# Third feed-forward: the rows of four fixed expert quads go through DRAM instead of through products of zeros and ones

## The chip, the core and the metric

The kernel runs on one core of one Trainium2 chip. The metric is the device time of one execution in microseconds; the median of three runs is compared. The engines are PE (matrix products; PEld loads its weights), DVE (vector), ACT (scalar and activation), POOL (GpSimd, which also issues the gathers and scatters by index) and SP (which issues most loads).

## What is computed

Four layers, each a cross-attention with a context and then a feed-forward, on 512 tokens of 256 features, all in float32. The change is in the feed-forward of the third layer, a mixture of eight experts in which each token goes to the one with the highest score:

```python
x = hidden_states.reshape(-1, 256)              # 512 tokens, normed
route = jax.nn.sigmoid(x @ router_w)            # 8 experts
max_ind = jnp.argmax(route, axis=1)
max_prob = jnp.take_along_axis(route, max_ind[:, None], axis=1)
for e in range(8):
    mask = (max_ind == e)[:, None]
    h = jax.nn.silu(x @ gate_w[e]) * (x @ up_w[e])          # inner width 512
    out = out + jnp.where(mask, h @ down_w[e], 0.0)
out = out * max_prob
# and around it: x = x + tanh(g_ffn[2]) * out
```

The fourth layer's cross-attention and feed-forward follow, and read x.

## The kernel before

**Slots.** The tokens of the third feed-forward are put into 768 slots, six quads of 128. Quads 0 to 3 (slots 1 to 512) are the fixed ones: each expert owns 64 slots, two blocks of 32, whatever the routing. Tokens beyond an expert's 64 go to blocks of 32 in quads 4 and 5, whose experts (`owners`) are only known when the counts are. `slot` holds each token's slot number from 1 on. Gathering tokens into slots is a product of a matrix of zeros and ones (`there`) with the normed tokens (L1233).

**A quad.** `l2_up(q)` does the gate and up products (L1396: four blocks of 32 rows side by side, 32 matmuls), silu on ACT (L1403) and the hidden product on DVE (L1405). `l2_turn` transposes the hidden rows (L634) and copies them out of PSUM (L195 on DVE and L197 on ACT in turn). `l2_down(q)` does the down products (L1417, 32 matmuls) into a PSUM tile `acc2`. `dn2` and `gu2` hold the eight down and eight gate-up weights; `home(q, j)` says which one a block uses.

**Back to tokens.** `l2_down` cuts the result into two parts[...]: DVE masks off the low bits (L1425), ACT copies the upper part (L1427), DVE takes the difference (L1428). `l2_mask(q)` (L1433) compares the row of slot numbers with the quad's own slots, which gives a matrix of zeros and ones; `l2_back(q)` (L1441) multiplies it with both parts, eight matmuls a quad, and all six quads accumulate into the two PSUM tiles `y`. `l3_stats(n)` then adds `y` times `c2` (the probability times the layer's gate) to row tile n of x on DVE (L276, the helper `add_to_x`) and starts the next norm.

**Order.** The loop over q runs up(q), mask and down of q - 1, turn of q, back of q - 2. The products on PE keep the order of the text (`inline(..., pe_line)`). DVE's order list was cleared just before this stage (`line.clear()`), so on DVE, ACT, POOL and SP a scheduler that runs at build time orders the instructions by the text and by when it takes their inputs to be ready; `behind(i, j, ...)` forces i after j on one engine. Each engine then executes its own list strictly in order, and waits at the head of it.

**Loads.** The weights of quads 4 and 5 overwrite those of the fixed quads: after up(q) SP loads the gate-up weights `gu2[2q]` and `gu2[2q+1]` (1 MB each, L1401), and after down(q) the down weights `dn2[2q]` and `dn2[2q+1]` (512 KB each, L1421). Then come the weights of the last feed-forward (`sh3`, `gu3`, `dn3`, L102) and its `shd` rows (L1476, L1477), which wait for a memset on POOL (L1475). Earlier, at 364.66 us, POOL writes zeros into the two DRAM tables `xg` and `yg` (L1038, L1039) that the last feed-forward uses to scatter (helper at L1635) and gather rows.

Of the kernel before, what the change touches and what calls it, by code (L numbers as in the profile page):

```python
# [17 lines left out]
F32 = mybir.dt.float32  # L18
F32R = mybir.dt.float32r
I32 = mybir.dt.int32  # L20
U8 = mybir.dt.uint8
AF = mybir.ActivationFunctionType
ALU = mybir.AluOpType
AX = mybir.AxisListType

P = 128
NT = 4
D = 256
# [9 lines left out]
QUADS = 6  # L38
# [12 lines left out]
def flamingo(ctx: ExitStack, tc: tile.TileContext, a: dict, out: bass.AP):  # L51
    nc = tc.nc

    def pool(name, bufs, space=None):
        kw = {} if space is None else {"space": space}
        return ctx.enter_context(tc.tile_pool(name=name, bufs=bufs, **kw))
# [3 lines left out]
    q2 = pool("q2", Q2)  # L60
    q1 = pool("q1", 4)
    small = pool("small", 6)
# [37 lines left out]
    def load(half, name):  # L100
        rows, cols = a[name].shape
        nc.sync.dma_start(half[0:rows, 0:cols], a[name])  # L102
        return half[0:rows, 0:cols]
# [67 lines left out]
    dram = pool("slots", 1, bass.MemoryType.DRAM)  # L171
    xg = dram.tile([E * CAP, D + 1], F32, name="xg")
    yg = dram.tile([2 * T, D], F32, name="yg")
    tg = const.tile([P, 8], F32, name="tg")

    nc.scalar.activation(tg[:, 0:1], eps_ln, AF.Sqrt)
# [8 lines left out]
    def behind(i, j, reason):  # L185

        tc.add_manual_dep(i.ins, j.ins.name, mybir.DependencyInfo(
            mybir.DependencyClass.NoSync, mybir.DependencyReason.DATA), reason=reason)
# [24 lines left out]
    def inline(i, line=line):  # L213
        if line:
            if line[-1] is not None:
                behind(i, line[-1], "in the order of the text")
            line[:] = [i]
        return i
# [49 lines left out]
    def mm(shape=None):  # L268
        return ps_mm.tile(shape or [P, 512], F32, tag="mm", name="mm")

    def chain(dst, pairs):
        for i, (lhsT, rhs) in enumerate(pairs):
            inline(nc.tensor.matmul(dst, lhsT=lhsT, rhs=rhs, start=(i == 0), stop=(i == len(pairs) - 1)), pe_line)  # L273

    def add_to_x(n, acc, scalar, cols=slice(0, D)):
        return inline(nc.vector.scalar_tensor_tensor(x[:, n, cols], acc, scalar, x[:, n, cols], ALU.mult, ALU.add))  # L276
# [202 lines left out]
    def l0_finish(n, den, mixed):  # L479
        r = q1.tile([P, D], F32, tag="q1", name="r0")  # L480
        inline(nc.vector.reciprocal(r, den))
        sums.append(mixed[:, 1, :])
        inline(nc.vector.tensor_mul(mixed[:, 0, :], mixed[:, 0, :], r))
        add_to_x(n, mixed[:, 0, :], gx(0))
        return r
# [4 lines left out]
    mixed, acc, es, stats, sums = {}, {}, {}, {}, []  # L490
    for s in range(18):
        n = s // 4
        if s < 16:
            es[s] = l0_scores(n, s // 2 % 2, s % 2)
        if 1 <= s <= 16:
            m, i, half = (s - 1) // 4, (s - 1) // 2 % 2, (s - 1) % 2
# [27 lines left out]
        if s % 4 == 1 and s > 1:  # L524
            den = l0_exchange(mixed[n - 1], n == 2, n == 4)
            r = l0_finish(n - 1, den, mixed[n - 1])
# [328 lines left out]
    for h in range(16):  # L855
# [9 lines left out]
        for b in range(B):  # L865
# [34 lines left out]
            if hl and g < 3:  # L900
                n = 2 * (hl - 1) + b
# [133 lines left out]
    zero = q2.tile([P, D + 1], F32, tag="q2", name="zero")  # L1035
    nc.gpsimd.memset(zero, 0.0)
    nc.gpsimd.iota(zero[:, D : D + 1].bitcast(I32), pattern=[[0, 1]], base=4096, channel_multiplier=0)
    nc.gpsimd.dma_start(xg.rearrange("(g p) d -> p g d", p=P), zero.unsqueeze(1).to_broadcast([P, E * CAP // P, D + 1]))  # L1038
    nc.gpsimd.dma_start(yg.rearrange("(g p) d -> p g d", p=P), zero[:, 0:D].unsqueeze(1).to_broadcast([P, 2 * NT, D]))  # L1039


    w2 = ffn1[3]
# [148 lines left out]
    def rtile(shape=(P, NT, E), dtype=F32):  # L1191
        return small.tile(list(shape), dtype, tag=f"r{len(shape)}", name="route", bufs=12)
# [37 lines left out]
    def gather2(dst, k, cols, tiles=range(NT)):  # L1230
        for n in tiles:
            for h in (xh, xl):
                inline(nc.tensor.matmul(dst, lhsT=h[:, n, k * P : (k + 1) * P], rhs=there[n][:, cols],  # L1233
                                        start=(n == 0 and h is xh), stop=(n == NT - 1 and h is xl)), pe_line)
# [99 lines left out]
    slot = rtile((P, NT))  # L1334
# [37 lines left out]
    c2 = const.tile([P, NT], F32, name="c2")  # L1372
    inline(nc.vector.tensor_scalar_mul(c2, top, gf(2)))
    line.clear()
    row = q2.tile([P, T], F32, tag="q2", name="row")

    def second_rows():
        p = mm([P, 2, SL - 512])
        for k in range(2):
            gather2(p[:, k, :], k, second)  # L1380
        for k in range(2):
            nc.scalar.copy(xsT[k][:, second], p[:, k, :])
        p = mm()
        chain(p, [(ones_r, diag.rearrange("p n t -> p (n t)"))])
        nc.scalar.copy(row, p)

    def home(q, j):

        return 2 * q + j // 2 if q < 4 else 4 * (q - 4) + j

    def l2_up(q):
        pa, pb = mm(), mm()
        for w, ps in ((0, pa), (1, pb)):
            for k in range(2):
                for j in range(4):
                    inline(nc.tensor.matmul(ps[j * BLK : (j + 1) * BLK, :],  # L1396
                                            lhsT=xsT[k][:, (4 * q + j) * BLK : (4 * q + j + 1) * BLK],
                                            rhs=gu2[home(q, j)][:, w * 1024 + k * 512 : w * 1024 + (k + 1) * 512], start=(k == 0), stop=(k == 1)), pe_line)
        if q < 4:
            for i in (2 * q, 2 * q + 1):  # L1400
                nc.sync.dma_start(gu2[i], a["l2_gu_all"][bass.ds(owners[i], 1), :, :].rearrange("e p c -> (e p) c"))  # L1401
        s = q2.tile([P, T], F32, tag="q2", name="silu")
        nc.scalar.activation(s, pa, AF.Silu)  # L1403
        h = q2.tile([P, T], F32, tag="q2", name="h2")
        nc.vector.tensor_mul(h, s, pb)  # L1405
        return h

    def l2_turn(h):
        hT = q2.tile([P, 4, P], F32, tag="q2", name="hT2")
        transposed(h, hT)  # L1410
        return hT

    def l2_down(q, hT):
        acc = ps_tr.tile([P, D], F32, tag="tr", name="acc2")
        for c in range(4):
            for j in range(4):
                inline(nc.tensor.matmul(acc[j * BLK : (j + 1) * BLK, :], lhsT=hT[:, c, j * BLK : (j + 1) * BLK],  # L1417
                                        rhs=dn2[home(q, j)][:, c * D : (c + 1) * D], start=(c == 0), stop=(c == 3)), pe_line)
        if q < 4:
            for i in (2 * q, 2 * q + 1):  # L1420
                nc.sync.dma_start(dn2[i],  # L1421
                                  a["l2_dn_all"][bass.ds(owners[i], 1), :, :].rearrange("e p c -> (e p) c"))

        top = q1.tile([P, D], F32, tag="q1", name="top2")
        nc.vector.tensor_scalar(top.bitcast(I32), acc.bitcast(I32), -4096, None, ALU.bitwise_and)  # L1425
        o = q2.tile([P, 2, D], F32R, tag="q2", name="o2")
        nc.scalar.copy(o[:, 0, :], top)  # L1427
        nc.vector.tensor_sub(o[:, 1, :], acc, top)  # L1428
        return o

    def l2_mask(q):
        back = q2.tile([P, T], F32R, tag="q2", name="back")
        nc.vector.tensor_scalar(back, row, own[:, q : q + 1], None, ALU.is_equal)  # L1433
        return back

    def l2_back(q, o, back, y):
        for n in range(NT):
            for i in range(2):


                inline(nc.tensor.matmul(y[n // 2][:, n % 2, :], lhsT=back[:, n * P : (n + 1) * P], rhs=o[:, i, :],  # L1441
                                        start=(q == 0 and n % 2 == 0 and i == 0),
                                        stop=(q == QUADS - 1 and n % 2 == 1 and i == 1)), pe_line)

    y = [ps_acc.tile([P, 2, D], F32, tag="acc", name="y2") for _ in range(2)]
    hTs, os, backs = {}, {}, {}
    for q in range(QUADS + 2):
        if q < QUADS:  # L1450
            h = l2_up(q)
        if q == 0:
            second_rows()
        if 1 <= q <= QUADS:
            backs[q - 1] = l2_mask(q - 1)
            os[q - 1] = l2_down(q - 1, hTs.pop(q - 1))

        if q == 4:
            w = pair(0, "sh3")
            sh = [load(w[:, k, :], f"l3_sh{k}") for k in range(2)]  # L1460
            w = pair(3, "gu3")
            gu3 = [load(w[:, k, :], f"l3_gu{k}") for k in range(2)]
        if q == 5:
            w = pair(4, "gu3")
            gu3 += [load(w[:, k, :], f"l3_gu{2 + k}") for k in range(2)]
            w = pair(5, "dn3")
            dn3 = [load(w[:, k, :], f"l3_dn{k}") for k in range(2)]
        if q < QUADS:
            hTs[q] = l2_turn(h)
        if q >= 2:  # L1470
            l2_back(q - 2, os.pop(q - 2), backs.pop(q - 2), y)
    pe_line.clear()
    late = pair(1, "late").rearrange("p s c -> p (s c)")
    shd = late[:, 0 : 6 * D].rearrange("p (c d) -> p c d", d=D)
# [310 lines left out]
    hs, hTs = {}, {}  # L1785
# [14 lines left out]
    rows = []  # L1800
    for n in range(NT):
        o = q2.tile([P, 2, D], F32, tag="q2", name="o3g")
# [680 lines left out]
```

## Time and profile before

| what | before |
|---|---|
| time, median of 3 runs (lowest to highest) | 583.55 us (582.22 to 584.46) |
| the profiled execution: its own time | 583.24 us |
| its span, first to last instruction | 581.5 us |
| mean granted clock of PE | 0.993 |
| busy in the span: PE, DVE, ACT, POOL | 550.4, 319.3, 229.9, 138.5 us |
| moved by DMA | 60.19 MB, 104 GB/s over the span |
| third feed-forward, first up product to first addition to x | 448.69 to 492.69 us |

A line of a profile names the engine, the line of the kernel, the operation and what it writes and reads (`out<-in`). In a timeline the first two numbers are start and duration in us, and a bracket at the end gives the idle time ahead of the instruction and what ended it. In the chain of waits each piece is what the next one waited for. GB/s stand in 40 equal slices of the span, 14.5 us each.

### The profile page before, as it was taken

How to read it: one execution, taken by the hardware profiler on the slowest of the kernel's cores; microseconds unless marked ns; L12 is line 12 of the kernel's file. 1: busy time of each engine (PE TensorE's matmuls, PEld its weight loads, DVE VectorE, ACT ScalarE, POOL GpSimd, SP SyncE). 2: the span in 40 equal slices, each digit the busy share in tenths (PEclk: the TensorE clock that was granted, in tenths of full speed). 3: DMA queues.
4: the chain of work that ended last, by engine and by line, in shares of the span. 5: the costliest groups of instructions: out<-in, count | busy, mean ns of one | idle time of the engine just before them, and what ended most of it. 6: DMA issues, size and time to landing. Idle time of an engine off the chain costs nothing.

```text
span 581.5 us, 8641 instructions
## 1 busy us (share of the span) xinstructions
PE 550.4 (95%) x3296; PEld 395.9 (68%) x3296; DVE 319.3 (55%) x731; ACT 229.9 (40%) x468; POOL 138.5 (24%) x233
## 2 busy tenths in 40 slices
PE   8988899989999999999999999999999999899995
PEld 6544575658888888788888887557766446884454
DVE  6979654284557455664545477314467434563323
ACT  6857544554344444534344531420332211432320
POOL 3887153131103011211101113102012000252150
PEclk9979999999999999999999999999999999999999
DMA  7900300000000400030003325932030799704013
GB/s 304 402 4 16 131 0 0 2 0 2 0 1 0 145 0 2 2 144 1 0 8 138 145 73 220 363 114 117 0 144 3 284 422 417 195 36 122 18 44 122
DMA packets 16071, 60.19 MB, mean 104 GB/s; under 512 B 2685, under 2 KB 5956, under 8 KB 12390
## 3 DMA queue, kind: packets, MB, share of 16 engines
q1 hardware_dynamic: 13974, 54.75, 25.4%
q0 software_dynamic: 1472, 4.28, 2.0%
q10 hardware_dynamic: 576, 0.53, 0.3%
q8 instruction: 28, 0.46, 0.3%
q14 instruction: 21, 0.17, 0.1%
HBM read 54.75 MB, written 5.25 MB: 103 GB/s over the span
## 4 chain that ended last, share of the span: by engine, by line
PE 74%; DVE 10%; POOL 5%; DMA 5%; ACT 3%; issue 2%; SPq 1%; POOLq 0%; ACTq 0%; DVEq 0%
PE mm L273 22%; PE acc L273 18%; PE mm L594 8%; PE mm L596 4%; PE mm L1396 4%; PE q L594 2%; PE mm L1729 2%; POOL tern L356 2%; PE acc L1417 2%; DMA w<-in_l_gate 2%; DVE x L276 1%; PE outT L680 1%; PE acc L1751 1%; PE q L596 1%; DVE signs L363 1%
## 5 line engine op out<-in xcount | busy, mean ns | idle before, releaser
L273 PE MATMUL mm<-qT,kT 128*128 128x256 f32 x256 | 61.0, 381 | 0.2 <-DVE kT L600 0.2
L273 PE MATMUL acc<-e,v 128*128 128x256 f32 x256 | 60.4, 379 | 0.0
L587 POOL TENSOR_TENSOR h_parts<-w,h_top 128x256 fp32r<-128x256 f32 x28 | 22.6, 808 | 150.9 <-PE acc L273 85.5
L273 PEld LDWEIGHTS mm<-qT,kT 128*128 128x128 f32 x256 | 48.0, 189 | 9.7 <-ACT oT L764 1.6
L273 PEld LDWEIGHTS acc<-e,v 128*128 128x128 f32 x256 | 48.4, 189 | 7.7
L753 ACT ACTIVATE e<-mm 128x512 f32<-128x512 f32 x64 | 38.0, 596 | 26.0 <-PE mm L273 25.8
L756 DVE TENSOR_TENSOR t<-e,e 128x512 f32<-128x512 f32 x32 | 22.1, 690 | 36.2 <-ACT e L753 36.2
L450 ACT ACTIVATE e<-s 128x512 f32<-128x512 f32 x64 | 33.0, 607 | 13.9 <-PE s L446 9.9
L227 POOL TENSOR_TENSOR rstd<-mv,eps_ln 128x1 f32<-128x1 f32 x30 | 6.2, 206 | 101.9 <-DVE mv L226 101.9
L273 PE MATMUL mm<-xT,ffn 128*128 128x512 f32 (+1 forms) x80 | 28.0, 509 | 1.3 <-ACT xT L1006 1.3
L273 PE MATMUL acc<-w,oT 128*128 128x256 f32 x112 | 27.2, 386 | 2.1 <-ACT oT L764 2.1
L594 PE MATMUL mm<-ctx_top,h_parts 128*128 128x512 f32 x56 | 27.2, 485 | 1.1 <-ACT h_parts L586 1.1
L599 ACT ACTIVATE v<-mm 128x512 f32<-128x512 f32 x24 | 14.3, 597 | 34.3 <-PE mm L596 34.3
L600 DVE SCALAR_TENSOR_TENSOR v<-mm,v 128x512 f32<-128x512 f32 x24 | 16.6, 691 | 18.7 <-ACT v L599 18.7
L276 DVE SCALAR_TENSOR_TENSOR x<-acc,gsum,x 128x256 f32<-128x256 f32 x56 | 24.1, 479 | 4.9 <-PE acc L273 4.9
L446 PE MATMUL s<-w_q,ctx_nat 32*128 32x256 f32 x256 | 23.9, 427 | 2.8 <-ACT e L450 2.0
L273 PEld LDWEIGHTS acc<-w,oT 128*128 128x128 f32 x112 | 20.7, 190 | 6.3 <-ACT oT L764 3.7
L599 ACT ACTIVATE kT<-mm 128x512 f32<-128x512 f32 x28 | 16.7, 598 | 20.6 <-PE mm L596 20.6
L764 ACT COPY oT<-acc 128x256 f32<-128x256 f32 x32 | 11.9, 373 | 32.4 <-PE acc L273 32.4
L273 PEld LDWEIGHTS mm<-xT,ffn 128*128 128x128 f32 x80 | 15.0, 190 | 13.6 <-issue 11.0
L594 PE MATMUL mm<-v_parts,ctx_top 128*128 128x512 f32 x48 | 22.1, 459 | 1.8 <-ACT e L753 1.8
L600 DVE SCALAR_TENSOR_TENSOR kT<-mm,kT 128x512 f32<-128x512 f32 x28 | 19.3, 689 | 7.1 <-ACT kT L599 7.1
(394 smaller groups left out, 1157.9 us busy)
## 6 DMA issues: line engine op xcount, KB each, us to landing
gu<-in_l_gu_all SPq DMA_DIRECT2D x16, 1024.0 KB, 7.0
w<-in_l_all SPq DMA_DIRECT2D x4, 2048.0 KB, 13.3
dn<-in_l_dn_all SPq DMA_DIRECT2D x4, 1024.0 KB, 6.3
dn<-in_l_dn_all SPq DMA_DIRECT2D x8, 512.0 KB, 9.7
gu<-in_l_gu SPq DMA_DIRECT2D x4, 704.0 KB, 11.7
ctx_nat<-in_ctx SPq DMA_DIRECT2D x4, 512.0 KB, 13.4
ctxT<-in_ctxT SPq DMA_DIRECT2D x4, 512.0 KB, 5.3
sh<-in_l_sh SPq DMA_DIRECT2D x2, 704.0 KB, 8.6
```

The source lines that it names most:

```text
L273: inline(nc.tensor.matmul(dst, lhsT=lhsT, rhs=rhs, start=(i == 0), stop=(i == len(pairs) - 1)), pe_line)
L276: return inline(nc.vector.scalar_tensor_tensor(x[:, n, cols], acc, scalar, x[:, n, cols], ALU.mult, ALU.add))
L446: in_turn(nc.tensor.matmul(ps[j][:, k, :], lhsT=ctx_nat[rows, b, hf, c * P : (c + 1) * P], rhs=qm[rows, n, i, :], start=True, stop=True))
L450: exps.append(nc.scalar.activation(es[j], ps[j], AF.Exp))
L587: nc.gpsimd.tensor_sub(dst[1], src, t)
L594: inline(nc.tensor.matmul(same, lhsT=left(i, k), rhs=right(i, k), start=(k == 0 and i == 0), stop=(k == 1 and i == 1)), pe_line)
L596: inline(nc.tensor.matmul(cross, lhsT=left(2, k), rhs=right(2, k), start=(k == 0), stop=(k == 1)), pe_line)
L599: nc.scalar.mul(dst, cross, -EPS * scale)
L600: return inline(nc.vector.scalar_tensor_tensor(dst, same, (1.0 + EPS) * scale, dst, ALU.mult, ALU.add))
L753: nc.scalar.activation(e, s, AF.Exp)
L756: nc.vector.tensor_add(t, es[0], es[1])
L1396: inline(nc.tensor.matmul(ps[j * BLK : (j + 1) * BLK, :], lhsT=xsT[k][:, (4 * q + j) * BLK : (4 * q + j + 1) * BLK], rhs=gu2[home(q, j)][: ...
```

## The change

The results of quads 0 to 3 no longer go back through masks and products. ACT copies each quad's `acc2` to SBUF, POOL writes its 128 rows (1 KB each) into a new DRAM table `ys`, and after the fourth quad POOL issues four gathers, one for each row tile of 128 tokens, by the index `static` (slot number less one; tokens without a fixed slot get row 512, which holds zeros). DVE adds the four gathered tiles to x with `add_to_x`, forced behind the hidden product of quad 5. Quads 4 and 5 keep masks and back products; back(4) is split in halves, one ahead of down(5) and one after it. The down loads of the last quads are moved in the text: four after down(2) and four after down(3), instead of two after each of the first four. The table's zero row is written beside the other zeros.

```diff
+    ys = dram.tile([5 * P, D], F32, name="ys")
...
+    nc.gpsimd.dma_start(ys[4 * P : 5 * P, :], zero[:, 0:D])
...
+    static = small.tile([P, NT], I32, tag="static", name="static", bufs=1)
+    nc.vector.tensor_scalar(static, slot, -1.0, 512.0, ALU.add, ALU.min)
...
-        nc.vector.tensor_mul(h, s, pb)
+        product[:] = [nc.vector.tensor_mul(h, s, pb)]
         return h
...
-        if q < 4:
-            for i in (2 * q, 2 * q + 1):
+        if q in (2, 3):
+            for i in range(4 * q - 8, 4 * q - 4):
                 nc.sync.dma_start(dn2[i],
                                   a["l2_dn_all"][bass.ds(owners[i], 1), :, :].rearrange("e p c -> (e p) c"))
+        if q < 4:
+            o = q1.tile([P, D], F32, tag="q1", name="o2s")
+            nc.scalar.copy(o, acc)
+            nc.gpsimd.dma_start(ys[q * P : (q + 1) * P, :], o)
+            return
...
+    def static_rows():
+        for n in range(NT):
+            r = q2.tile([P, D], F32, tag="q2", name="y2s")
+            nc.gpsimd.indirect_dma_start(out=r, out_offset=None, in_=ys[:, :],
+                                         in_offset=bass.IndirectOffsetOnAxis(ap=static[:, n : n + 1], axis=0),
+                                         bounds_check=5 * P - 1, oob_is_err=False)
+            fixed.append(r)
...
-    def l2_back(q, o, back, y):
-        for n in range(NT):
+    def l2_back(q, o, back, y, tiles=range(NT)):
+        for n in tiles:
             for i in range(2):
...
-                                        start=(q == 0 and n % 2 == 0 and i == 0),
+                                        start=(q == 4 and n % 2 == 0 and i == 0),
...
-    for q in range(QUADS + 2):
+    for q in range(QUADS + 1):
         if q < QUADS:
             h = l2_up(q)
         if q == 0:
             second_rows()
+        if q == QUADS:
+            l2_back(4, os[4], backs[4], y, (0, 1))
         if 1 <= q <= QUADS:
-            backs[q - 1] = l2_mask(q - 1)
+            if q > 4:
+                backs[q - 1] = l2_mask(q - 1)
             os[q - 1] = l2_down(q - 1, hTs.pop(q - 1))
+            if q == 4:
+                static_rows()
...
+        if q == 5:
+            for n, r in enumerate(fixed):
+                behind(add_to_x(n, r, c2[:, n : n + 1]), product[0], "rows come late")
         if q < QUADS:
             hTs[q] = l2_turn(h)
-        if q >= 2:
-            l2_back(q - 2, os.pop(q - 2), backs.pop(q - 2), y)
+        if q == QUADS:
+            l2_back(4, os[4], backs[4], y, (2, 3))
+    l2_back(5, os[5], backs[5], y)
     pe_line.clear()
```

## The prediction

> **What bounds the kernel now.** I read the page's engine table first, then the slices, then the chain of waits through the stage that the change touches, and last the instructions and transfers of that stage.
>
> ```profile
> PE 550.4 (95%) x3296; PEld 395.9 (68%) x3296; DVE 319.3 (55%) x731; ACT 229.9 (40%) x468; POOL 138.5 (24%) x233
> ...
> GB/s 304 402 4 16 131 0 0 2 0 2 0 1 0 145 0 2 2 144 1 0 8 138 145 73 220 363 114 117 0 144 3 284 422 417 195 36 122 18 44 122
> ```
>
> PE is busy nearly everywhere, but the three slices of 284, 422 and 417 GB/s (451 to 494 us) are this stage, and there the transfers are full too. Two resources run at their limit at once; a step taken off one helps only as far as the other allows. The chain through the stage (start, duration, what):
>
> ```profile
> 466.88 0.95 PE y L1441 x8
> 467.83 3.57 PE mm L1396 x32
> 471.40 1.73 PE acc L1417 x32
> 473.13 0.58 PE tr L634 x4
> 473.71 0.95 PE y L1441 x8
> ...
> 480.55 0.95 PE y L1441 x8
> 481.50 3.75 PE mm L1396 x31
> ...
> 485.28 0.20 PE mm L1396
> 485.48 1.93 PE acc L1417 x28
> 487.41 0.59 PE tr L634 x4
> 487.99 0.95 PE y L1441 x8
> 488.94 1.86 PE acc L1417 x32
> 490.81 1.15 PE y L1441 x8
> 491.95 0.12 PE tr L1489 x2
> 492.07 0.59 PE y L1441 x4
> 492.69 0.50 DVE x L276
> ```
>
> A quad is 3.57 (up) + 1.73 (down) + 0.59 (turn) + 0.95 (back) us of PE without a gap. The last quad's up takes 3.75 + 0.20 instead of 3.57, and the timeline names why: its last weights had only just landed.
>
> ```profile
> 482.06 2.28 PEld L1396 LDWEIGHTS mm<-gu,xsT 128*32 128x32 f32 x25 [0.48 <-DMA gu<-in_l_gu_all]
> ```
>
> So PE has no more than about half a microsecond over the weights. The stage ends at 492.69 us, when DVE adds the first finished row tile to x; everything later follows from that moment. I price the change by where this moment goes.
>
> **What is removed.** The back products of quads 0 to 3: 32 matmuls, 4 x 0.95 = 3.8 us, all on the chain. On DVE four masks (0.48), four cuts and four differences (0.42 each), 5.3 us; DVE idles over 4 us before each hidden product, so that is worth nothing. The ACT cast (0.41) becomes a copy of the same size: nothing.
>
> **What PE alone would do.** Without the three backs ahead of it the chain reaches up(5) early: up(3) 466.88 to 470.45, down(2) to 472.2, turn to 472.8, up(4) to 476.3, down(3) to 478.1, turn to 478.7, against 481.50 now (2.85 us).
>
> **The weights that move.** All eight down loads of the last two quads (0.33 to 0.50 us of SP each) now stand behind the gate-up loads of quads 2 and 3: four after down(2), four after down(3); no load goes. Bytes, at the 0.42 MB/us of the full slices, with 1.7 us from issue to first data (issue 452.36, data from about 454.1): gu(4,5), issued at 464.6 as now, flows 466.3 to 471.3. gu(6,7), issued at 470.45, flows 472.2 to 477.2. The four first down loads (2.1 MB), issued at 472.2, end at 482.2, the last four at 487.2. The new traffic shares the same engines: four writes and four gathers of 131 KB, 1.05 MB or 2.5 us. I give 0.8 us of it to the loads ahead of down(4) (483) and all to the last (490). So up(5) no longer waits, but down(4) starts at 483 instead of 482.2, and down(5) has no weights before 490, where today it starts at 488.94. The 3.8 us of PE are eaten here: even with nothing else late, down(5) runs 490 to 491.9, its cut and difference (from the end of down(5) at 490.8 to 491.8 today, 1.0 us) give 492.8, half a back (0.59) gives 493.4: +0.7. If SP keeps today's order of readiness instead (the loads of 304.07 us went out ahead of loads that stand before them in the text), gu(7) lands at 482 as now plus up to 1 us for the writes: between -0.3 and +0.7. I take +0.7.
>
> **The added path.** Quad 3's rows go: down(3) ends 478.1, ACT copy 0.41, POOL issue at 478.6, landing, then four gathers that wait for it, one every 1.28 us (the scatters of 518.96, 520.26, 521.53 us), landing, then four additions on DVE (0.48 to 0.50 each). The unknown is the landing of a POOL transfer in saturated engines. On quiet engines scatters of the same 128 rows land in:
>
> ```profile
> xg<-late,goes POOLq DMA_INDIRECT x8, 2.7
> ```
>
> The upper end is the 1 MB of zeros at 364.66, beside gate-up loads:
>
> ```profile
> yg<-zero POOLq DMA_DIRECT2D x1, 1024.0 KB, 13.8
> ...
> q0 software_dynamic: 563, 2.23, 57.8%
> q1 hardware_dynamic: 581, 1.67, 43.2%
> ```
>
> The last two lines are the 10 us from 371: the software queue got more than half of full engines, so it isn't starved, and most of the 13.8 us are eight times the rows. The landing is nearer the low end. **The rule:** the Trainium skill, page "DMA: Bandwidth & Descriptors", section "Anatomy of one DMA — SWDGE (gpsimd) path", fits 2.0 us + bytes/436 GB/s, 2.3 us here; its section "Latency and other measured facts" puts memory access at 0.2 us on average but 2 us at high load, which would make it about 4.1 (estimate of mine from the two). By the first alone: write 480.9, last gather issued 484.9, landed 487.2, rows in x by 487.7. By the second, and by the trace's 2.7 plus a share of the load, I take 4.0: write 482.6, gathers issued 482.7 to 486.5, last landing 490.5, rows in x by 491.1. The loaded value decides, since the slices say 420 GB/s throughout. No row shows a gather; it is bounded by 2.4 us (fastest scatter) and 8 (half the zeros' time, with something over).
>
> **What waits behind it.** The additions are held only behind the hidden product of quad 5 (about 483.1). Nothing in the code holds them behind the cut of down(4), and the program's order on an engine is by readiness in places: the product of L1489 stands after the last back in the text and runs ahead of it at 491.95; POOL's copy of L1568 ran at 487.73, ahead of norms that precede it. So I expect DVE to meet at least some additions before the cut of quad 4. DVE then stands until the rows land. Behind it: cut and difference of quad 4 (491.1 to 492.0), PE's first half of back(4) (0.48, to 492.5), which the new text puts ahead of down(5), so down(5) to 494.35, cut and difference to 495.35, half a back to 495.95. Against 492.69 that is **+3.3 us**. If the additions stand behind the difference of quad 4, they finish at 491.1 beside the wait for weights: the +0.7 above.
>
> **At nothing.** One index instruction on DVE (0.17 us, like L1345) in a gap. One more zero transfer (about 1.0 us of POOL, 128 KB): POOL idles 27.60 us from 366.8. The first three row writes (1 us of POOL each): POOL idles 43.8 us here. The memset L1475 and, after it, SP's load of shd move behind the gathers, from 487.5 to at most 488; its rows are first read at 564.4 (the shared products of L273), over 70 us of cover. If POOL's gathers ran past 495, norms of the next stage would wait up to 5.1 us (4 x 1.28): that is in the third case.
>
> **The rivals.** (1) DVE stands ahead of quad 4's cut: +3.3, from +1.2 (landing 3.2) to +6.5 (5.5). For: the gaps filled by readiness. Against: text order puts the cut first. It decides once the last row lands after about 487. (2) Additions after quad 4's difference, weights the limit: -0.4 to +2.5, centre +0.7. For: 422 GB/s. (3) The software queue is slow under load, 6 to 8 us a landing, twice in a row: +7 to +11. For: 13.8 us for the zeros. Against: 57.8% of the engines. (4) The other side: the saving arrives. The additions stay out of the way and loads keep ahead (the first down loads fill the gap at 460 us and gu(6,7) comes before the rest), so down(4) ends 484.0, back(4) follows at 484.9, down(5) 485.4 to 487.3, first addition at 488.8: -3.9, or -1.5 if the last down loads land at 487. It decides as soon as 1 us less of loads than today's lies ahead of each down. Against: the sum of bytes, which grows. A change that leaves the back products in place is excluded by the diff: the products start at quad 4.
>
> **How the numbers follow.** The sum is against the profiled execution, span 581.5, 583.24 us with what lies around it; the median of the three runs is 583.55, 0.3 above. 583.55 + 3.3 = 586.9. Chances: case 1 0.58 (0.46 of it above +2.9 us, which is 0.5%, about what a measurement of this kernel can tell from no change), case 2 0.22, case 3 0.10, case 4 0.10 (0.07 beyond 0.5%). Slower 0.46 + 0.10 = 0.56; same 0.12 + 0.22 + 0.03 = 0.37; faster 0.07. The range runs from just below case 2 (-1.0, 582.5) to the near part of case 3 (+8.5, 592.0); outside lie most of case 4 and half of case 3. Case 1 alone would be 584.7 to 590.
>
> **What the profile after would show.** Right: 16 back matmuls on L1441's successor, not 48; up(5) starting near 478.7 without a wait for gu; DVE's first addition of a fetched row waiting for the gather for several microseconds, with cut and difference of quad 4 after it; PE idle ahead of the first half of back(4); the first addition of y near 496. Wrong: landings of 2.7 us in the full stretch, or the cut of quad 4 ahead of the additions (then case 2); a wait of PE on the down weights longer than on DVE (case 2 too); landings over 6 us (case 3); the first addition of y before 490 (case 4).

## The result and the profile after

| | before | after |
|---|---|---|
| first comparison, median (lowest to highest) | 584.0 us of 4 (582.22 to 593.93) | 602.88 us of 4 (600.16 to 604.7) |
| ratio | | 1.03 [1.0255, 1.0345] |
| side by side later, median | 588.56 us of 31 (582.38 to 593.37) | 600.92 us of 4 (599.51 to 604.7) |
| ratio | | 1.0218 [1.0156, 1.028] |
| profiled execution, and its span | 583.24 us, 581.5 us | 602.28 us, 600.5 us |
| granted clock of PE in it, mean | 0.993 | 0.970 |

The change is slower by 2 to 3%, 12.4 us between the medians side by side, where +3.3 us was forecast. Medians here are over all runs, while ratios leave out runs more than 1.5% above the fastest of their kernel. One execution of the kernel before takes anywhere from 582 to 596 us, so each experiment is compared with runs of the kernel before beside it, and stages by the time since their first up product.

The page of the changed kernel: engine table, then the granted clock and the transfers in 40 slices of 15.0 us.

```profile
PE 556.9 (93%) x3264; PEld 397.7 (66%) x3264; DVE 317.0 (53%) x724; ACT 230.0 (38%) x468; POOL 145.6 (24%) x242
...
PEclk9978999989999999999999999999989996899999
...
GB/s 302 383 3 26 116 0 1 1 0 2 1 0 62 79 1 1 2 140 1 1 141 140 71 76 368 213 141 0 80 61 148 379 412 332 75 19 135 18 40 119
```

PE has 32 products fewer, as the diff says, and yet is "busy" longer (556.9 against 550.4 us): products took longer at the lower clock (0.970 against 0.993). The clock row has a 6 and an 8 in the slices that begin at 495 and 510 us, at the end of and just after the three full slices of transfers (379, 412, 332).

The chain of waits of the changed kernel through the stage (start, duration, what):

```profile
483.92 5.45 DMA ys<-o2s
...
490.24 0.41 POOL y2s L1445
...
492.98 1.00 POOL y2s L1445
493.98 0.30 issue
494.28 7.08 DMA y2s<-ys,static
501.36 0.02 issue
501.38 0.06 DVE x L277
...
501.79 0.43 DVE top L1436
...
502.75 1.22 PE y L1460 x4
...
505.49 2.42 PE acc L1423 x28
...
509.68 0.50 DVE x L277
```

The chain no longer runs through PE: write of quad 3's rows, gathers, landing of the last gather, the fourth addition, and only then the cut of quad 4. The first addition of y (the last line) stands 55.89 us after the first up product, before 44.0. What PE and DVE did meanwhile, from the timeline of the changed kernel (idle time ahead and its releaser in brackets), PE first, then DVE, and last the same cut of quad 4 in the kernel before:

```profile
483.68 3.64 PE L1400 MATMUL mm<-gu,xsT 128*32 128x512 f32 x32
...
488.52 0.62 PE L1423 MATMUL acc<-dn,hT 128*32 128x256 f32 x2 [0.78 <-DMA dn<-in_l_dn_all]
489.91 1.91 PE L1423 MATMUL acc<-dn,hT 128*32 128x256 f32 x26 [0.77 <-DMA dn<-in_l_dn_all]
...
502.75 1.22 PE L1460 MATMUL y<-o,back 128*128 128x256 f32 x4 [10.34 <-ACT o L1438]
```

```profile
496.89 0.48 DVE L277 SCALAR_TENSOR_TENSOR x<-y2s,c,x 128x256 f32<-128x256 f32 x1 [8.32 <-DMA y2s<-ys,static]
...
501.79 0.41 DVE L1436 TENSOR_SCALAR top<-acc 128x256 int32<-128x256 int32 x1
```

```profile
487.44 0.42 DVE L1425 TENSOR_SCALAR top<-acc 128x256 int32<-128x256 int32 x1 [0.57 <-PE acc L1417]
```

The accumulator of quad 4 was complete at 491.8 us. DVE could not cut it for ten microseconds, since the additions of fetched rows stand at the head of its list; PE stood for 10.34 us behind that. Up(5) starts without a wait for its weights, and down(4) does wait for its own. The landings, from the groups of the two tiles (gathers, then writes):

```profile
DMA to landing us min/median/max: 6.2/6.4/7.1
...
DMA to landing us min/median/max: 5.4/6.0/6.7
```

Most of a landing is waiting and not moving: quad 3's write was issued at 483.92, up to 487.7 only the loads' queue moved packets (1.57 MB), and its own packets then left within 1.2 us (487.72 to 488.95).

And the granted clock in two windows, the first chosen on the stretch that ran at half (busy times, then clock, DMA share, GB/s):

```profile
496.32:506.56 10.24, 3.81 (x22) 2.22 (x26) 3.42 (x9) 0.89 (x2) 0.00 (x0) 0.50 1.04 373
...
506.56:513.39 6.83, 3.76 (x35) 2.35 (x28) 4.34 (x13) 0.78 (x2) 1.64 (x5) 1.00 0.88 187
```

The half-speed stretch begins 3.9 us after PE's last product before the gap and ends 3.8 us after it has products again; down(5), which lies in it for the most part, took 3.99 us instead of 1.94 before.

### The profile page after: what moved, and what is told of

The parts are those of the page before. It is cut to its first block, busy times and chain, and to the rows that moved or that the text cites. A ratio compares the mean times of both kernels' runs of the same rounds, so it can differ in the third digit from the quotient of the medians.

```text
span 600.5 us, 8597 instructions
## 1 busy us (share of the span) xinstructions
PE 556.9 (93%) x3264; PEld 397.7 (66%) x3264; DVE 317.0 (53%) x724; ACT 230.0 (38%) x468; POOL 145.6 (24%) x242
## 4 chain that ended last, share of the span: by engine, by line
PE 75%; DVE 9%; DMA 5%; POOL 4%; ACT 3%; issue 3%; SPq 0%; POOLq 0%; ACTq 0%; DVEq 0%
PE mm L274 25%; PE acc L274 17%; PE mm L595 8%; PE mm L597 4%; PE mm L1400 2%; PE q L595 2%; PE mm L1757 2%; POOL tern L357 2%; DMA w<-in_l_gate 2%; DVE x L277 2%; PE acc L1423 1%; PE outT L681 1%; PE acc L1779 1%; DMA y2s<-ys,static 1%; PE q L597 1%
## 5 line engine op out<-in xcount | busy, mean ns | idle before, releaser
L600 ACT ACTIVATE kT<-mm 128x512 f32<-128x512 f32 x28 | 16.8, 599 | 20.5 <-PE mm L597 20.5
L765 ACT COPY oT<-acc 128x256 f32<-128x256 f32 x32 | 11.9, 373 | 32.4 <-PE acc L274 32.4
L447 PEld LDWEIGHTS s<-w_q,ctx_nat 32*128 32x128 f32 x256 | 15.7, 206 | 11.4 <-issue 5.5
```

The lines of the kernel that those rows point to most:

```text
L447: in_turn(nc.tensor.matmul(ps[j][:, k, :], lhsT=ctx_nat[rows, b, hf, c * P : (c + 1) * P], rhs=qm[rows, n, i, :], start=True, stop=True))
L600: nc.scalar.mul(dst, cross, -EPS * scale)
```

## The experiments

Stages below are us since the first up product. "Rows added" is the span of the four additions of fetched rows.

| kernel | cut of quad 4 | rows added | down(5) from, to | first, last addition of y | ratio to before |
|---|---|---|---|---|---|
| before | 38.75 | none | 40.18, 42.12 | 44.0, 47.82 | 1 |
| the change | 47.99 | 43.1 to 48.1 | 50.1, 54.09 | 55.89, 59.72 | 1.03 |
| the change, second profile | 48.3 | 42.87 to 48.4 | 50.42, 55.57 | 57.37, 61.2 | 1.0218 |
| additions where x is read | 38.19 | 44.03 to 50.4 | 39.83, 43.19 | 44.98, 50.40 | 1.008 |
| rows from SBUF | 37.47 | 34.69 to 36.4 | 39.12, 42.47 | 44.25, 48.07 | 1.003 |
| last loads after the gathers | 44.09 | 41.7 to 44.2 | 46.2, 51.36 | 53.16, 56.99 | 1.0153 |

**The change again.** No edit; the changed kernel beside the kernel before.

> The changed kernel once more beside the kernel before on the same chip. In its profile the first addition of y to x stood 55.9 us after the first up product, 44.0 in the kernel before: 11.9 us of the 19 us between the two spans; 5.1 us lie ahead of the stage, in code that is the same, where stretches of PE at half clock stood (0.970 against 0.993 on average). If those belong to the run and not to the change, the clocks of the two come nearer here and the difference is 12 to 16 us; if they belong to the change, it stays 18 to 20 us.

Measured: 600.92 against 588.56 us, 1.0218 [1.0156, 1.028]. In its profile (599.78 us) the stage begins at 448.79 us, before at 448.69: what was added ahead of the stage (index, zero row) shows as no more than 0.1 us, and the 5.1 us by which the first profile after was late there lay in identical code, with four half-speed stretches of 3.41 us on the way (at 49, 124, 438 and 449 us) that neither this profile nor that of the kernel before has. The first addition of y is 13.4 us later than before, and a second half-speed stretch of 6.83 us follows at 59.5. Thus 13.4 and about half of 6.83 make 16.8 us, against 16.5 between this profiled execution and the one before.

**Additions where x is read.** Each row tile is added just ahead of y's addition to it, held behind the difference of quad 5; nothing else changes.

```diff
-        if q == 5:
-            for n, r in enumerate(fixed):
-                behind(add_to_x(n, r, c2[:, n : n + 1]), product[0], "rows come late")
...
     def l3_stats(n):
+        behind(add_to_x(n, fixed[n], c2[:, n : n + 1]), difference[0], "where x is read")
         add_to_x(n, y[n // 2][:, n % 2, :], c2[:, n : n + 1])
```

> The same, but each fetched row tile is added right before y is added to the same tile of x, behind the difference of quad 5. Theory (DVE stands at the head of its queue for the rows, ahead of the cut of quad 4): the cut of quad 4 follows down(4) at once, the wait for the rows moves to the end and runs beside down(5); first addition of y 45 to 48 us after the first up product, time 9 to 12 us below the changed kernel. Rival (the late down weights hold PE, the rows are beside): at most 3 us below it. Rival (the clock): no gain, the clock stays at 0.97.

Measured: 591.95 against 588.56 us, 1.008 [1.0047, 1.0114], 9 us under the changed kernel beside it. DVE's timeline:

```profile
489.92 0.42 DVE L1436 TENSOR_SCALAR top<-acc 128x256 int32<-128x256 int32 x1 [3.41 <-issue]
...
495.77 0.47 DVE L277 SCALAR_TENSOR_TENSOR x<-y2s,c,x 128x256 f32<-128x256 f32 x1
496.72 0.48 DVE L277 SCALAR_TENSOR_TENSOR x<-y,c,x 128x256 f32<-128x256 f32 x1 [0.47 <-PE y L1460]
...
497.80 0.46 DVE L277 SCALAR_TENSOR_TENSOR x<-y2s,c,x 128x256 f32<-128x256 f32 x1
498.29 0.48 DVE L277 SCALAR_TENSOR_TENSOR x<-y,c,x 128x256 f32<-128x256 f32 x1
```

The cut follows down(4) at once; no addition waits for a gather, though these land no sooner (5.9 to 7.5 us). So the slow landings cost what they did through the place of the additions in DVE's list, and through the gap of PE that followed from it, which is gone too (0.48 us ahead of the first half of back(4)). What is left has a place too: each addition is 0.5 us of DVE in the row of norms, and y's additions come 1.6 to 2.0 us apart instead of 1.1 to 1.4, so that the last is 2.6 us later than before. The rest of the 3.4 us between the medians is not placed.

**Rows from SBUF.** The four copies are added straight from SBUF; no write, no gather. The rows are added in slot order and not by token; the additions are of the same number and size.

```diff
-            o = q1.tile([P, D], F32, tag="q1", name="o2s")
+            o = q2.tile([P, D], F32, tag="q2", name="o2s")
             nc.scalar.copy(o, acc)
-            nc.gpsimd.dma_start(ys[q * P : (q + 1) * P, :], o)
+            fixed.append(o)
             return
...
-            if q == 4:
-                static_rows()
```

> The writes and gathers are left out: the four copies in SBUF are added to x in slot order, so rows reach the wrong tokens; all else as in the changed kernel. Theory: without the rows' landing DVE never stands; what is left is PE without four backs, with the moved loads: first addition of y 41 to 45 us after the first up product, time from 3 us below to 1 us above the kernel before. If the loads' new order were the main cost, PE would still wait over 3 us for down weights and the first addition stay above 48 us.

Measured: 589.5 against 588.56 us, 1.003 [0.999, 1.0069]. Without the whole path through DRAM the change wins nothing, although 32 products are gone. PE's timeline names the reason at down(4), and PEld's at down(5):

```profile
489.33 0.62 PE L1423 MATMUL acc<-dn,hT 128*32 128x256 f32 x2 [0.22 <-DMA dn<-in_l_dn_all]
490.61 1.91 PE L1423 MATMUL acc<-dn,hT 128*32 128x256 f32 x26 [0.66 <-DMA dn<-in_l_dn_all]
...
495.71 1.43 PEld L1423 LDWEIGHTS acc<-dn,hT 128*32 128x32 f32 x26 [0.43 <-DMA dn<-in_l_dn_all]
```

Up(5) ended as early as in the changed kernel, but down(4) took 4.0 us in three pieces and down(5) 3.4 us, at full clock. Down(4) stood for its weights. Down(5) stood for them for 0.43 us and was also split, after its first four products, by another product of PE's list (L1515), which in the kernel before stands behind down(5).

The additions ran ahead of the cut here too, in the wait for down(4), and cost nothing, since their data were there.

**Old order of loads.** As above, with the down loads after each of the first four quads as in the kernel before (rows again in slot order).

```diff
-        if q in (2, 3):
-            for i in range(4 * q - 8, 4 * q - 4):
+        if q < 4:
+            for i in (2 * q, 2 * q + 1):
```

> As e2_no_dram (rows added from SBUF in slot order, no writes or gathers), with the eight down loads back at their old places, two after each of the first four downs. In e2_no_dram PE stood about 2 us in down(4) and the first addition of y came at 44.25 us, no earlier than before. Theory (the weights' bytes are the limit, so the order only moves the wait): up(5) waits for gate-up weights instead, first addition of y 43 to 44.5. Rival (the new order of loads eats the saving): no wait in down(4), first addition of y at 41 to 42, time 2 to 3 us below the kernel before.

Measured: 589.96 against 589.43 us, 1.0018 [0.9989, 1.0047]. The wait has moved into up(5), which took from 29.88 to 37.44, and the first addition of y came at 45.24, 0.7 us past the forecast range:

```profile
487.75 1.04 PE L1400 MATMUL mm<-gu,xsT 128*32 128x512 f32 x2 [0.37 <-DMA gu<-in_l_gu_all]
490.26 3.19 PE L1400 MATMUL mm<-gu,xsT 128*32 128x512 f32 x25 [1.47 <-DMA gu<-in_l_gu_all]
```

**Without the down loads.** Rows from SBUF in slot order, and the eight down loads (4.2 MB) left out as well, so that quads 4 and 5 use the down weights of the fixed experts.

```diff
-        if q in (2, 3):
-            for i in range(4 * q - 8, 4 * q - 4):
-                nc.sync.dma_start(dn2[i],
-                                  a["l2_dn_all"][bass.ds(owners[i], 1), :, :].rearrange("e p c -> (e p) c"))
```

> As e2_no_dram, and the eight down loads of the last two quads are left out too, so these quads use the fixed experts' down weights. Theory (the weights' bytes eat the saving of PE): no wait in down(4) or down(5), first addition of y at 39.5 to 41.5 us after the first up product instead of 44.25, time 2.5 to 4.5 us below the kernel before. If something else than the loads holds PE, it stays at 43 to 44.

Measured: 587.69 against 588.97 us, 0.9977 [0.994, 1.0014]: the time can't be told from no change, so the expected 2.5 to 4.5 us aren't shown. The stage tells more. Up(5) and down(4) run through,

```profile
488.16 3.64 PE L1400 MATMUL mm<-gu,xsT 128*32 128x512 f32 x32
491.62 1.91 PE L1423 MATMUL acc<-dn,hT 128*32 128x256 f32 x32
```

and the first addition of y stands at 41.36, 2.6 us ahead of the kernel before and 2.9 ahead of the same kernel with its loads. That is about the 2.85 us that PE alone had saved at up(5). Down(5) took 1.93 us here and was not split; of the 2.9 us some 1.0 go with that (3.35 - 1.93 - 0.43, an estimate). With the old order of loads down(5) was not split either and took 1.93 us too, so that pair differs by the loads alone: 45.24 against 41.36, 3.9 us. The granted clock was 1.00 from the first up product to the first addition of y in all these profiles (before, rows from SBUF, old order, no down loads). So the bytes of the weights take the saving away, in either order of the loads.

**Last loads after the gathers.** The loads of the last feed-forward (`sh3`, `gu3`, `dn3`) wait for the gathers.

```diff
-        nc.sync.dma_start(half[0:rows, 0:cols], a[name])
+        i = nc.sync.dma_start(half[0:rows, 0:cols], a[name])
+        for g in gathers_all:
+            tc.add_manual_dep(i.ins, g.ins.name, mybir.DependencyInfo(mybir.DependencyClass.Sync, mybir.DependencyReason.DATA),
+                              reason="behind the gathers")
```

> As the changed kernel, but the loads of the last feed-forward (sh3, gu3, dn3, 5.8 MB) wait until the four gathers have landed, so that only down loads share the engines with the rows. If load on the engines makes the landings long (write 5.5 us, gathers up to 7.1), the gathers land in 2.5 to 4 us here and the first addition of y comes 50 to 53 us after the first up product. If a gather of rows from DRAM takes 6 to 7 us in itself, nothing changes (55 to 57).

Measured: 598.84 against 588.56 us, 1.0153 [1.0076, 1.0231]. The landing of the gathers from the group of `y2s`, and PE's timeline (line numbers are 5 or 6 higher here):

```profile
DMA to landing us min/median/max: 3.1/3.6/5.2
```

```profile
496.64 1.22 PE L1466 MATMUL y<-o,back 128*128 128x256 f32 x4 [6.33 <-ACT o L1443]
...
499.32 3.63 PE L1428 MATMUL acc<-dn,hT 128*32 128x256 f32 x28
```

With those loads out of the way a gather lands in 3.6 us instead of 6.4 (medians): it is the load of the engines, not the gather itself. The writes, which meet the down weights, still took 5.5 to 6.7; no run takes the loads away from them, so that load makes them slow too is argued and not shown. The cut comes 3.9 us sooner than in the changed kernel, the first addition of y only 2.7: PE's gap of 6.33 us was long enough for a half-speed stretch of 10.24 us, and down(5) took 5.2. That the time falls below that of the changed kernel (600.92) is not shown, with four runs of each.

**PE kept at work.** Useless products fill PE's gap ahead of the first half of back(4), first 22 of them, then 11 (each of the 22 took 0.87 us).

```diff
         if q == QUADS:
+            filled = mm()
+            for _ in range(11):
+                inline(nc.tensor.matmul(filled, lhsT=ident, rhs=xsT[0][:, 0:512], start=True, stop=True), pe_line)
             l2_back(4, os[4], backs[4], y, (0, 1))
```

> The changed kernel with 22 products of no use (identity times gathered tokens, about 0.44 us each) on PE between the turn of quad 5 and the first half of back(4), where PE stood idle for over 10 us. Theory (the idle stretch makes the granted clock fall to half, which then slows down(5), the backs and the products that follow): the clock stays full there, down(5) takes 2 us and not 4 to 5, the time falls 4 to 7 us below the changed kernel (601). If the half clock had another cause, the time stays within 1 us of it.

> As e5_pe_fill, whose 22 products took 0.87 us each and ran 19 us, so that they set the end themselves (the clock did stay full and down(5) took 1.94 us). Now 11 of them, 9.5 us, which end about when the cut of quad 4 comes. Theory (the idle stretch costs clock): down(5) 2 us, first addition of y at 52 to 54 us after the first up product, time 4 to 7 us below the changed kernel (601). If the clock is not what costs, the time stays at 600 to 602.

Measured with 22: 608.02 us, 1.0363 [1.0292, 1.0434]. They took 19.05 us in place of the gap's ten and set the end themselves: they had been estimated at half of what they took. The clock stayed full, and down(5) took 1.94 us. With 11, from PE's timeline:

```profile
487.93 9.61 PE L1476 MATMUL mm<-xsT,ident 128*128 128x512 f32 x22
497.95 0.74 PE L1460 MATMUL y<-o,back 128*128 128x256 f32 x4 [0.42 <-ACT o L1438]
498.62 1.93 PE L1423 MATMUL acc<-dn,hT 128*32 128x256 f32 x32
```

The cut of quad 4 is where it was (47.79), so DVE's wait is untouched, but down(5) runs at full clock and the first addition of y comes at 53.18, 2.7 and 4.2 us before the two profiles of the changed kernel. Within the stage this is the clock's share of the loss. In the runs it didn't show: the profiled one took 594.63 us, but the median of four is 601.99 (1.029 [1.0229, 1.0351]), at mean clocks from 0.972 to 0.990. Whether the filling lowers the time of the whole kernel stays open.

**Two mends together, and more.** Additions where x is read and last loads after the gathers, in one kernel; then the same with two of the down loads back after down(0); then that with POOL scaling and adding the rows, and back(4) whole behind down(5).

```diff
-        if q in (2, 3):
-            for i in range(4 * q - 8, 4 * q - 4):
+        if q in (0, 2, 3):
+            for i in {0: (0, 1), 2: (2, 3, 4, 5), 3: (6, 7)}[q]:
...
+                for n, r in enumerate(fixed):
+                    nc.gpsimd.tensor_scalar(r, r, c2[:, n : n + 1], None, ALU.mult)
+                    nc.gpsimd.tensor_add(x[:, n, :], x[:, n, :], r)
...
-            l2_back(4, os[4], backs[4], y, (2, 3))
+            l2_back(4, os[4], backs[4], y)
```

> Additions where x is read (as in e1_adds_at_use) and the loads of the last feed-forward after the gathers (as in e3_loads_after_gathers). In e3 the last row had landed by 43.2 us, so DVE waits for no row here; down weights remain. First addition of y 43 to 44.5, time within 2 us of the kernel before (e1 alone: 3.4 us above). If each of the two only hid the other's cost, it stays 2 us or more above.

> As v1_both, and the first two down loads stand after down(0) again, where the transfers had a gap; the other six stay behind the gate-up loads. Theory (bytes): 1 MB less lies ahead of down(4), which then waits 0 to 1 us, first addition of y at 41.5 to 43, time 0 to 2.5 us below the kernel before. If PE's wait only moves to down(5) or to up(5), it is at 43 to 44.5 as in v1_both.

> As v2_both_early_down, but POOL scales the fetched rows and adds them to x, so that DVE neither waits for them nor spends 0.5 us on each in the row of norms at the end, and back(4) stands whole behind down(5), so that PE doesn't wait for quad 4's difference. In e1, v1 and v2 the additions of y came every 1.9 us instead of 1.4. Theory: 1.4 us again, first addition of y at 42.5 to 44.5 us, time 1.5 us below to 1 us above the kernel before. If POOL is too slow (four times two operations, with the norms' two behind them), the norms wait and it is 1 to 4 us above.

Measured: 593.06 (1.005 [1.0006, 1.0095]) and 592.84 us (1.0038 [0.9999, 1.0077]) against 589.43, and 594.42 us (1.0123 [1.0064, 1.0182]) against 588.97. In the first, y's last addition is at 50.28, as with the additions alone (50.40): the row of norms on DVE is the limit by then. In the second the two early loads only brought back the wait of up(5):

```profile
485.94 3.19 PE L1405 MATMUL mm<-gu,xsT 128*32 128x512 f32 x25 [1.25 <-DMA gu<-in_l_gu_all]
```

In the third, POOL's timeline and one line of DVE's:

```profile
502.45 0.92 POOL L1486 TENSOR_SCALAR y2s<-y2s,c 128x256 f32<-128x256 f32 x1
503.45 0.72 POOL L1487 TENSOR_TENSOR x<-x,y2s 128x256 f32<-128x256 f32 x1
...
504.79 0.58 POOL L234 TENSOR_TENSOR rstd<-rstd,less_half 128x1 f32<-128x1 f32 x1
```

```profile
505.40 0.41 DVE L238 TENSOR_SCALAR xn<-x,mv,rstd 128x256 f32<-128x256 f32 x1 [3.44 <-POOL rstd L234]
```

POOL also computes the norms' `rstd`, and its eight new operations (6.6 us in all) run ahead of the first of them. DVE waits 3.44 us, PE 6.52, and half clock follows for 10.24 us. None of the three is faster than the kernel before. Their medians lie 3.4 to 5.5 us above it, each above its forecast.

## Why the prediction was wrong

**What PE alone would do: right.** Up(5) was put 2.85 us earlier; it starts at 29.88 against 32.74.

**The weights that move: right in kind, short in size.** Down(4) was to start at 483, 34.3 after the first up product, and so to end at 36.2. It started at 33.34 on what had landed and stood for the rest, to 38.02. That the bytes eat the saving holds: with rows from SBUF it is +0.25 us at the first addition of y (44.25 against 44.0), where the prediction had +0.7. The other-side case, the saving arriving, is refuted by the two kernels with rows from SBUF, and appears once the bytes are left out (2.6 us).

**What waits behind: right.** DVE met the additions ahead of quad 4's cut and stood there. Holding them behind quad 5's difference instead brought the cut from 48 back to 38.2.

**The size of the wait: the step that failed.** The rows were to be in x at 491.1, which is 42.4 after the first up product; in the profile after they are at 48.06. The terms, with the profile that answers each:

| term of the sum | prediction | profile after | difference |
|---|---|---|---|
| write issued, since first up product | 29.9 | 30.1 | 0.2 |
| landing of the write | 4.0 | 5.45 | 1.45 |
| to the first gather | 0.1 | 0.87 | 0.8 |
| four gathers, first to last issue | 3.84 | 4.04 | 0.2 |
| landing of the last gather | 4.0 | 7.08 | 3.1 |
| last addition | 0.6 | 0.5 | -0.1 |

Together 5.6 us, of which 4.5 are the two landings. The value of 4.0 stood on the trace's quiet 2.7 us plus a share of the load and on an estimate of 4.1; what spoke against more was a share of the engines: the software queue had 57.8% in a full stretch of the kernel before, "so it isn't starved". But a share of bytes says what a queue moves, not how long one small transfer takes to come through beside others: here it had 9.4% of the engines' time between 476 and 505 us and its transfers of 128 rows took 5.4 to 7.1 us: quad 3's write stood 3.8 us and the first gather 4.4 us before its first packet left. The Trainium skill, page "DMA: Bandwidth & Descriptors", section "Anatomy of one DMA — SWDGE (gpsimd) path", fits a time from which I estimate 2.3 us for these bytes, and my estimate with the latency at high load was 4.1; neither holds under about 400 GB/s of loads, where the measured values decide. Holding back the last feed-forward's loads (3.6 us) shows the cause for the gathers, 3.1 us of the sum; for the write's 1.45 the cause stays open. In the prediction these long landings had a case to themselves, at 0.10, which asked for them "twice in a row". They need not be two separate draws: both fell into the same stretch of full engines (403 GB/s from 485 to 505 us). And the case was set apart from the one in which DVE stands ahead of the cut; what happened is both at once. The ends of that first case don't follow from its own sum either: 3.2 and 5.5 us for each landing give +1.7 and +6.3, not +1.2 and +6.5.

**What was not priced: PE's clock.** The forecast case itself had PE idle for some 6.5 us ahead of back(4), and took back, down(5) and back at their durations at full clock: 4.9 us from the cut of quad 4 to the first addition of y. It was 7.9 us in the first profile after and 9.1 in the second, against 5.25 before. The Trainium skill, page "TensorE: Matmul & The Clock Gate", section "Part 1: The HAM clock gate (the "warmup" mystery)", says that about 3.4 us without work take the clock to half and that about as much work brings it back, in free-running windows of 3413 ns. The four profiles with a gap of over 6 us agree in kind: half speed in stretches of 10.24 or 13.65 us, three and four such windows. The times differ: half speed began 2.6 to 3.9 us after the last product, in two of the four within 3.0 us, and ended 3.8 us after the first product in the first profile after, but 6.5 to 6.9 us in the other three. With PE kept busy in the gap (11 products) the 7.9 became 5.4.

The sum closes: +3.3 predicted, 5.6 for the landings and what lies between, 3.0 from the cut to the first addition (2.5 of it the clock, by the run with 11 products), 11.9 us; measured at the first addition of y 55.89 - 44.0 = 11.9 us. The rest of the 19.0 us between the two profiled executions is 5.1 us ahead of the stage, in code that the change leaves alone and not found in the second profile, and about 1.7 us of a half-speed stretch of 3.41 us behind it.

**At nothing: held.** Up(0) is 0.1 us late in the second profile; the writes on POOL were issued on time (30.1); the shared rows' load was not on the chain.

## What to carry to other kernels

An operation that waits for a transfer belongs, on an engine that executes in order, behind all work whose inputs come earlier; name that order explicitly, since a forced predecessor that is merely early enough lets it go ahead of the rest, and moving the additions alone was worth 9 us. Where two resources are full at once, as PE and the loads here, price a removed step by what it gives with the other resource unchanged: with all of the DRAM path gone, 32 products fewer were worth nothing; with the weights' bytes gone too they were worth 2.6 us in the stage, and still no time that could be told from the noise. When a forecast leaves PE idle for 6 us or more, charge half clock for what follows (10 to 14 us of it here), and take the landing of a small transfer from a stretch with the same load, not from a quiet one or from a share of the bytes.

## What the runs showed of the hardware

- A POOL-issued transfer of 128 rows of 1 KB landed in 2.7 us on quiet engines (median of eight scatters in the kernel before), gathers in 2.9 to 5.2 with the last feed-forward's loads held back, and writes and gathers in 5.4 to 7.6 beside some 400 GB/s of loads. Under these loads the first packet of quad 3's write left 3.8 us after its issue (483.92 to 487.72); on the quiet engines of the kernel before, the first scatter's left 1.7 us after it (517.54 to 519.23).
- A gap of PE of 6.3 to 10.3 us was followed in each of the four profiles that have one (the change twice, last loads after the gathers, POOL's additions) by 10.24 or 13.65 us at half clock, from 2.6 to 3.9 us after the last product on. Half clock also came in stretches of 3.41 or 6.83 us without such a gap, among others at about the same places of code that is the same in all kernels (123 to 132 and 433 to 456 us). Over 105 runs of the kernel before, a mean clock of 0.990 or more went with a median of 584.0 us (27 runs) and one of 0.980 to 0.984 with 590.0 (47). Why some executions have these stretches and others don't is not tested.
- On POOL the scaling of 128x256 floats took 0.92 to 0.94 us and the addition 0.72 to 0.74, against 0.48 for both in one operation on DVE.
